# Part of the first statistics moved from VectorE to ScalarE: one ring piece of each of the last four images

## The chip, the cores and the metric

The kernel runs on one core of a Trainium2 chip. The core has five engines with a queue each: TensorE (PE in the profile; PEld is its weight load), VectorE (DVE), ScalarE (ACT), GpSimd (POOL) and SyncE (SP, which here only issues transfers). Every engine works through its own list in order and waits on semaphores for the others. On-chip memory is SBUF (128 partitions) and PSUM, where TensorE writes. The metric is the device time of one execution in microseconds; lower is better.

## The reference

The input `x` is 16 images of 128 channels and 64x64 pixels, in fp32. Two layers follow each other:

```
def _gn(v, G=32, eps=1e-5):                 # group norm: 4 channels a group
    g = v.reshape(B_, G, C_ // G, H_, W_)
    m = mean(g, axis=(2, 3, 4)); s = var(g, axis=(2, 3, 4))
    return ((g - m) / sqrt(s + eps)).reshape(v.shape)

x = x + diagonal_lstm(_gn(x))
x = x + quantum_conv(_gn(x))
```

The diagonal LSTM skews each image, so that row i starts i columns later, and scans the columns: the gates of a row at one step come from its own input, from its own hidden state and from that of the row above. The second layer maps the 128 channels of each pixel to 4 angles, simulates a 4-qubit circuit, and maps 4 expectations back to 128 channels. What matters here is the first `_gn`: before the scan can begin, the mean and the variance of each image's groups must be known, over all of `x`.

## The kernel before

**Stages.** In a first stage (to about 104 us) all of `x` is read once and its statistics are taken, while the weights are transposed and a small recurrence for rows that still wait is run. The second stage is the scan, some 1200 us. The third computes the second layer and writes the output.

**Pieces.** An image's 4096 pixels a channel are cut into eight pieces of 512. Five go into the tile `ring`, where the scan needs them; three go into passing buffers, `rest` (three buffers) and `spare[0..3]`, only to be summed. `rows(b)` issues the five transfers, `behind(b)` the three, all on SyncE's queue. At turn `b` of the loop over images (L369 on) `rows(b + 2)` and `behind(b + 1)` are issued.

**Statistics.** `statistics(b, k)` is one `bn_stats` on VectorE over piece `k` of image `b` (L283). It writes six numbers into `stats[:, b, k]`: count, mean and sum of squared deviations, for two halves. `aggregated(b)` (L286) joins the eight sixes of an image into a mean and a variance, `mv1[:, b]`. At turn `b` VectorE takes the five ring pieces of image `b + 1`, then the three passing pieces of image `b`, then the aggregate of `b`.

**The waiting rows.** Rows of the image to which the skewed scan has not come yet see no input, but their gates have a bias, so their state moves in a known way, the same for each such row. `inv_step(j)` computes one step of that, 33 in all, two or three a turn: four TensorE products (L194), four activations on ScalarE (L197), three small GpSimd operations (L200 to L202), two more activations (L204, L205), which give `hinv`. Each step waits for the one before. After each, two `keep` products (L177) are issued, whose results nobody reads; they only keep TensorE working.

**The end of the stage.** GpSimd copies columns of `hinv` into `hst[0]`, the scan's first hidden state (L398, L399). TensorE then runs the scan's first products on it (L404), three more `keep` products on buffers of the last images, and then `group_mean`, a product of the means with a group-averaging matrix (`gm`, L142). VectorE turns that into `mean1` (L143), `var1` follows, a second product (`gv`, L422), and `inverse_root` gives `rstd1` (with a square root on ScalarE, L149, whose table is loaded before it). With these GpSimd normalises the first scan inputs (L564 to L574).

**Buffers.** `spare` is eight tiles of 128x512. `spare[0..3]` hold weights and then passing pieces, `spare[4..5]` are `xns`, the normalised inputs of even and odd scan steps, `spare[6..7]` are `hst`. All four of the last are zeroed on GpSimd early in the stage:

```
for v in (*hst, *xns, none):
    nc.gpsimd.memset(v, 0.0)
```

**What sets the order.** The whole stage is under a manual schedule: each engine runs its instructions in the order in which the code writes them; only the waits are put in by the framework.

Of the kernel before, what the change touches and what calls it, by code (L numbers as in the profile page):

```python
# [11 lines left out]
F32 = mybir.dt.float32  # L12
AF = mybir.ActivationFunctionType
# [3 lines left out]
P = 128  # L17
NB = 16
# [7 lines left out]
BLOCK = ROWS * NW  # L26
CHUNK = 2 * BLOCK
# [53 lines left out]
def kernel(  # L81
# [16 lines left out]
    nc = tc.nc  # L98
# [10 lines left out]
    ring = const.tile([P, RING // ROWS, NB, BLOCK], F32, name="ring")  # L109
# [11 lines left out]
    mean2 = const.tile([P, NB], F32, name="mean2")  # L121
    rstd2 = const.tile([P, NB], F32, name="rstd2")
# [3 lines left out]
    spare = [const.tile([P, CHUNK], F32, name=f"spare{i}") for i in range(8)]  # L126
# [8 lines left out]
    def block(r):  # L135

        return (r + AHEAD if r < SLOTS else r - SLOTS) // ROWS
# [17 lines left out]
    small = ctx.enter_context(tc.tile_pool(name="small", bufs=2))  # L155
    with ExitStack() as scan:
# [5 lines left out]
        bias = wpool.tile([P, 4], F32, name="bias")  # L162
# [4 lines left out]
        xns, hst = ([v.rearrange("p (q n) -> p q n", q=2) for v in spare[i : i + 2]] for i in (4, 6))  # L167
        none = state.tile([P, NB], F32, name="none")
        gates = scan.enter_context(tc.tile_pool(name="gates", bufs=1))
        spool = scan.enter_context(tc.tile_pool(name="spool", bufs=1))  # L170
        stats = spool.tile([P, NB, NG2, 6], F32, name="stats")
        ps_small = scan.enter_context(tc.tile_pool(name="ps_small", bufs=1, space=PSUM))

        def keep(pool, tag, v):

            ps = pool.tile([P, v.shape[-1]], F32, name=nc.get_next_instruction_name(), tag=tag)
            nc.tensor.matmul(ps, lhsT=wsT[:, 0:P], rhs=v, start=True, stop=True)  # L177
# [8 lines left out]
        def inv_step(j, pool):  # L186


            ps = {}
            rhs = hinv[:, j : j + 1].to_broadcast([P, P])  # L190
            for g in ORDER:
                ps[g] = pool.tile([P, P], F32, name=f"inv_ps{j}_{g}", tag=f"inv{g}")
                w = wsT[:, g * 128 : (g + 1) * 128]
                nc.tensor.matmul(ps[g], lhsT=w, rhs=rhs, start=True, stop=True)  # L194
            ac = small.tile([P, 4], F32, name=f"inv_a{j}", tag="inv_a")
            for g in ORDER:
                nc.scalar.activation(ac[:, g : g + 1], ps[g][:, 0:1], FUNC[g], bias=bias[:, g : g + 1])  # L197
            ig = small.tile([P, 2], F32, name=f"inv_i{j}", tag="inv_i")
            c = cinv[:, j + 1 : j + 2]
            nc.gpsimd.tensor_mul(ig[:, 0:1], ac[:, GF : GF + 1], cinv[:, j : j + 1])  # L200
            nc.gpsimd.tensor_mul(ig[:, 1:2], ac[:, GI : GI + 1], ac[:, GG : GG + 1])
            nc.gpsimd.tensor_add(c, ig[:, 0:1], ig[:, 1:2])  # L202
            th = small.tile([P, 1], F32, name=f"inv_t{j}", tag="inv_t")
            nc.scalar.activation(th, c, AF.Tanh)  # L204
            nc.scalar.activation(  # L205
                hinv[:, j + 1 : j + 2], th, AF.Identity, scale=ac[:, GO : GO + 1]
            )
# [7 lines left out]
        with ExitStack() as prep:  # L215
# [15 lines left out]
            post_n = pp.tile([P, 4], F32, name="post_n")  # L231
            ident = pp.tile([P, P], F32, name="ident")
            mv1 = pp.tile([P, NB, 2], F32, name="mv1")
            bias8 = pp.tile([P, 8], F32, name="bias8")
            co = gates.tile([P, 8, 8], F32, name="co")
            cur = gates.tile([P, 2, 16], F32, name="amp_in")
# [6 lines left out]
            def rows(b):  # L243
                for k in ORDERED:
                    at = (2 * k * ROWS - AHEAD) * NW if k else SLOTS * NW
                    nc.sync.dma_start(
                        out=ring[:, 2 * k : 2 * k + 2, b, :],
                        in_=xv[b, :, at : at + CHUNK].rearrange("c (k n) -> c k n", n=BLOCK),
                    )

            def behind(b):
                rests[b] = []
                for i, k in enumerate(range(RING * NW, NH * NW, CHUNK)):
                    n = (3 * b + i) % 7
                    if n < 3:
                        rest = rest_pool.tile([P, CHUNK], F32, name=f"rest{b}_{k}", tag="rest")
                    else:
                        rest = spare[n - 3]
                    nc.sync.dma_start(out=rest, in_=xv[b, :, k : k + CHUNK])
                    rests[b].append(rest)  # L260
# [20 lines left out]
            def statistics(b, k):  # L281
                v = ring[:, 2 * k : 2 * k + 2, b, :] if k < 5 else rests[b][k - 5]
                nc.vector.bn_stats(stats[:, b, k, :], v)  # L283

            def aggregated(b):
                nc.vector.bn_aggr(  # L286
                    mv1[:, b, :], stats[:, b, 0:8].rearrange("p g s -> p (g s)")
                )
# [19 lines left out]
            def coefficients():  # L308
                nc.gpsimd.tensor_mul(co[:, 0], trig[:, 0, 0, :], trig[:, 0, 2, :])
                nc.gpsimd.tensor_mul(co[:, 1], trig[:, 1, 0, :], trig[:, 0, 2, :])  # L310
                nc.gpsimd.tensor_mul(co[:, 2], trig[:, 0, 1, :], trig[:, 1, 2, :])
                nc.gpsimd.tensor_mul(co[:, 3], trig[:, 1, 1, :], trig[:, 1, 2, :])
                nc.gpsimd.tensor_scalar_mul(co[:, 4:8], co[:, 0:4], -1.0)
                nc.gpsimd.tensor_copy(cur[:, 0], expand)
                nc.gpsimd.memset(cur[:, 1], 0.0)


            def transposed(name, to, of):
                tp = ps_prep.tile([P, 512], F32, name=f"{name}_ps", tag="tp")
                for g in range(4):  # L320
                    nc.tensor.transpose(tp[:, g * 128 : (g + 1) * 128], of(g), ident)
                nc.scalar.copy(to, tp)
# [30 lines left out]
            for k in (1, 2):  # L353
                statistics(0, k)
            for i in range(2):
                v = ws_n[i]
# [1 line left out]
            transposed("wsT", wsT, lambda g: sum_n[:, g, :])  # L358
            biases()
            coefficients()  # L360
            for v in (*hst, *xns, none):
                nc.gpsimd.memset(v, 0.0)
            nc.gpsimd.memset(w_image, 0.0)

            for k in (3, 4, 0):
                statistics(0, k)


            between = [angle_weights, output_weights]  # L369
            done = 0  # L370
            for b in range(NB):
                while b < NB - 1 and done * (NB - 1) < EARLY * (b + 1):
                    inv_step(done, ps_inv)
                    keep(ps_keep, "keep", ring[:, 2, b, 0:P])
                    keep(ps_keep, "keep", wsT[:, 0:P])
                    if done == 0:

                        transposed("wxT", wxT, lambda g: wx_n[:, g, :])
                        transposed("w0T", w0T, lambda g: ws_n[g // 2][:, g % 2, 0::2])
                        transposed("w1T", w1T, lambda g: ws_n[g // 2][:, g % 2, 1::2])  # L380
                    elif done > 4 and between:
                        between.pop(0)()
                    done += 1
                if b + 2 < NB:
                    rows(b + 2)
                if b + 1 < NB:
                    behind(b + 1)
                    for k in ORDERED:
                        statistics(b + 1, k)
                for k in (5, 6, 7):  # L390
                    statistics(b, k)
                aggregated(b)
            prep_ps.close()


            ps_gate = scan.enter_context(tc.tile_pool(name="ps_gate", bufs=7, space=PSUM))
# [468 lines left out]
        with tc.manual_schedule():  # L865
# [26 lines left out]
            v = ring[:, block(NH - ROWS)].rearrange("p i (r w) -> p i r w", w=NW)[:, :, :, NW - STRIP :]  # L892
            d, sq = (work.tile([P, NB, ROWS, STRIP], F32, name=f"strip{i}", tag=f"both{i}") for i in range(2))
            m = mean2.unsqueeze(2).unsqueeze(3).to_broadcast([P, NB, ROWS, STRIP])
# [7 lines left out]
            m = small.tile([P, NB], F32, name="m2", tag="gn_m")  # L902
# [84 lines left out]
    def sines(b, c=None):  # L987

        if b not in turns:
            turns[b] = sinp.tile([P, CHUNK], F32, name=f"y{b}", tag="y")  # L990
        y = half(turns[b], c)
        nc.scalar.activation(y, ths[b, c], AF.Identity, bias=b_image[:, b : b + 1])  # L992
        near = half(nearp.tile([P, CHUNK], F32, name=f"near{b}_{c}", tag="near"), c)
        nc.vector.tensor_scalar(near, y, ROUND, ROUND, ALU.add, ALU.subtract)  # L994
        nc.vector.tensor_sub(y, y, near)  # L995
        yield
        nc.scalar.activation(y, y, AF.Sin, scale=TWO_PI)
# [67 lines left out]
    with tc.manual_schedule():  # L1065
# [18 lines left out]
        later = sines(1)  # L1084
# [8 lines left out]
        later = sines(2)  # L1093
# [6 lines left out]
        for b in range(1, NB):  # L1100
            po = outputs(b, 0)
            later = sines(b + 2) if b + 2 < NB else iter(())
# [50 lines left out]
```

## Time and profile before

| | us |
|---|---|
| median of 3 runs (lowest, highest) | 1413.59 (1413.12, 1415.5) |
| the profiled execution | 1412.49 |
| its span, first to last instruction | 1410.7 |
| busy in the span: PE, DVE, ACT, POOL | 1352.7, 980.5, 778.7, 921.3 |
| busy from 20 to 95 us: PE, DVE, ACT, POOL | 59.01, 72.42, 45.51, 18.31 |
| moved from 20 to 95 us | 370 GB/s |

The table's first three rows are times of whole executions; the profile's span is that of its own execution, 1.79 us shorter than its time. Busy time is the sum of what an engine executed; issuing of transfers, waits and branches don't count. In an order-of-time view a line gives start, duration, engine, line of the code, operation, output and inputs by name with their shapes, how many instructions were joined, and in brackets how long the engine was idle before and what ended that.

### The profile page before, as it was taken

The numbers are of one execution on the slowest core, as the hardware profiler recorded it, in microseconds if no ns is written. First come the engines' busy times: TensorE is split into PE (matmuls) and PEld (weight loads), VectorE is DVE, ScalarE is ACT, GpSimd is POOL, SyncE is SP. The second block draws the span as 40 slices with busy tenths as digits, with TensorE's granted clock in tenths as the row PEclk, the third lists the DMA queues.
The fourth block names the chain that finished last, engine by engine and source line by source line (L and its number), as shares of the span: only waits on it lengthen the run. The fifth ranks groups of instructions, "written<-read, shape, count | busy, mean of one in ns | idle before, by whom it ended". The sixth has DMA issues, their size and how long they took to land. (4 is left out here: it accounts for less than half of the span.)

```text
span 1410.7 us, 20301 instructions
## 1 busy us (share of the span) xinstructions
PE 1352.7 (96%) x6030; PEld 962.4 (68%) x6030; DVE 980.5 (70%) x2549; ACT 778.7 (55%) x1860; POOL 921.3 (65%) x1823
## 2 busy tenths in 40 slices
PE   6778999999999999999999999999999999989996
PEld 5658887777777666666777777777767778786332
DVE  7993565566665666787777776766665566876996
ACT  4555666555555555555555555555555566654331
POOL 4226887777777667778888876777777667763300
PEclk9999999999999999999999999999999999999998
DMA  9980000000000000133333100000000000004999
GB/s 325 368 287 2 1 1 1 1 1 1 0 1 1 0 1 1 60 120 120 119 121 120 60 1 1 0 1 1 1 1 0 1 1 1 1 31 135 389 405 354
DMA packets 78926, 107.06 MB, mean 76 GB/s; under 512 B 5552, under 2 KB 53712, under 8 KB 78816
## 3 DMA queue, kind: packets, MB, share of 16 engines
q1 hardware_dynamic: 74176, 94.39, 19.2%
q0 software_dynamic: 3408, 10.58, 2.0%
q8 instruction: 48, 0.79, 0.2%
q10 hardware_dynamic: 1232, 0.80, 0.2%
q14 instruction: 62, 0.51, 0.1%
HBM read 59.61 MB, written 46.14 MB: 75 GB/s over the span
## 5 line engine op out<-in xcount | busy, mean ns | idle before, releaser
L583 PE MATMUL ps<-spare,wxT 128*128 128x512 f32 (+18 forms) x1280 | 479.6, 517 | 0.7 <-POOL spare L574 0.7
L767 DVE TENSOR_TENSOR ps<-ps,both 128x256 f32<-128x256 f32 (+9 forms) x544 | 221.6, 408 | 305.1 <-PE ps L752 303.7
L771 ACT ACTIVATE ps<-ps,bias 128x512 f32<-128x512 f32 (+23 forms) x480 | 279.3, 583 | 220.2 <-DVE ps L767 183.7
L752 PE MATMUL ps<-spare,w1T 128*128 128x256 f32 (+16 forms) x1272 | 345.8, 353 | 9.8 <-DVE spare L834 4.9
L583 PEld LDWEIGHTS ps<-spare,wxT 128*128 128x128 f32 x1280 | 230.9, 190 | 173.2 <-issue 155.5
L752 PE MATMUL ps<-spare,w0T 128*128 128x256 f32 (+16 forms) x1272 | 343.8, 352 | 0.8 <-POOL spare L608 0.8
L802 ACT COPY both<-ps 128x256 f32<-128x256 f32 (+9 forms) x544 | 191.6, 355 | 180.8 <-PE ps L752 161.2
L617 POOL TENSOR_TENSOR ring<-ring,spare 128x256 f32<-128x256 f32 (+8 forms) x487 | 247.8, 540 | 31.2 <-DVE stats L705 21.1
L752 PEld LDWEIGHTS ps<-spare,w1T 128*128 128x128 f32 x1272 | 229.8, 190 | 35.7 <-DVE spare L834 7.6
L752 PEld LDWEIGHTS ps<-spare,wsT 128*128 128x128 f32 x1088 | 194.9, 190 | 86.3 <-DVE spare L834 34.7
L752 PE MATMUL ps<-spare,wsT 128*128 128x256 f32 (+14 forms) x1088 | 241.3, 365 | 5.4 <-DVE spare L834 3.6
L752 PEld LDWEIGHTS ps<-spare,w0T 128*128 128x128 f32 x1272 | 230.3, 190 | 22.1 <-POOL spare L608 0.9
L574 POOL TENSOR_TENSOR spare<-spare,rstd 128x512 f32<-128x512 f32 (+10 forms) x160 | 171.0, 1069 | 14.8 <-DVE rstd L153 2.3
L569 POOL TENSOR_TENSOR spare<-ring 128x256 f32<-128x256 f32 (+8 forms) x213 | 147.2, 701 | 0.0
L828 ACT ACTIVATE g<-cst 128x256 f32<-128x256 f32 (+20 forms) x320 | 103.0, 368 | 64.3 <-DVE cst L827 63.7
L834 DVE TENSOR_TENSOR spare<-g,ps 128x256 f32<-128x256 f32 (+17 forms) x319 | 105.4, 368 | 44.0 <-ACT g L828 42.1
L564 POOL TENSOR_TENSOR spare<-ring,mean 128x16 f32<-128x16 f32 (+8 forms) x247 | 130.9, 539 | 6.2 <-DVE mean L143 6.0
L608 POOL TENSOR_TENSOR spare<-spare 128x240 f32<-128x240 f32 (+9 forms) x136 | 102.7, 755 | 29.5 <-DVE spare L834 25.7
L771 ACT ACTIVATE g<-ps,bias 128x512 f32<-128x512 f32 (+20 forms) x160 | 97.4, 609 | 27.1 <-DVE ps L767 21.3
L854 POOL COPY spare<-spare 128x16 f32<-128x16 f32 x64 | 21.1, 330 | 134.1 <-DVE spare L834 134.1
L827 DVE TENSOR_TENSOR cst<-cst,ps 128x256 f32<-128x256 f32 (+20 forms) x320 | 104.3, 367 | 5.5
L824 DVE TENSOR_TENSOR ps<-ps,g 128x512 f32<-128x512 f32 (+20 forms) x160 | 95.1, 594 | 17.0 <-ACT g L771 16.6
(368 smaller groups left out, 1097.2 us busy)
## 6 DMA issues: line engine op xcount, KB each, us to landing
out_dram<-ring SPq DMA_DIRECT2D x94, 256.0 KB, 5.1
ring<-in_x_dram SPq DMA_DIRECT2D x80, 256.0 KB, 5.6
low<-ring SPq DMA_DIRECT2D x6, 2048.0 KB, 7.5
ring<-in_x_dram SPq DMA_DIRECT2D x6, 2048.0 KB, 8.1
spare<-in_x_dram SPq DMA_DIRECT2D x27, 256.0 KB, 5.5
rest<-in_x_dram SPq DMA_DIRECT2D x21, 256.0 KB, 5.6
ring<-low POOLq DMA_DIRECT2D x19, 256.0 KB, 7.0
out_dram<-spare SPq DMA_DIRECT2D x14, 256.0 KB, 6.0
```

The lines of the kernel that those rows point to most:

```text
L564: nc.gpsimd.tensor_sub(by_pairs(xn, 0, j, n), x0, over(mean1, n))
L569: nc.gpsimd.tensor_sub(by_pairs(xn, 1, j, n), lower, of)
L574: nc.gpsimd.tensor_mul(v, v, r)
L583: nc.tensor.matmul(ps[g][:, :, a:b], lhsT=wxT[:, g * 128 : (g + 1) * 128], rhs=xns[t % 2][:, :, a:b], start=t > 0, stop=True, skip_group_c ...
L617: engine.tensor_add(x1, x1, by_pairs(new, q, j, n))
L752: nc.tensor.matmul(out, lhsT=w[:, g * 128 : (g + 1) * 128], rhs=rhs, start=False, stop=True, skip_group_check=True,)
L767: nc.vector.tensor_add(v, v, both[g][:, a:b])
L771: nc.scalar.activation(to[:, :, a:w], ps[g][:, :, a:w], FUNC[g], bias=bias[:, g : g + 1])
L802: nc.scalar.copy(both[g][:, a:b], ps[g][:, 0, a:b])
L827: nc.vector.tensor_add(c[:, q], c[:, q], ig[:, q])
L828: nc.scalar.activation(th[:, q, a:w], c[:, q], AF.Tanh)
L834: nc.vector.tensor_mul(new[:, q, a:v], th[:, q, a:v], act[GO][:, q, a:v])
```

## The change

The first ring piece (k = 0) of images 12 to 15 is no longer taken by `bn_stats`. The new generator `beside(b)` has ScalarE pass over it twice, once with Identity and once with Square, each time of (m - x), where m is a mean that `bn_stats` found for piece 1 of the same image; the accumulator outputs, the sum and the sum of squares, go into a column of `mean2` and `rstd2`, tiles that are unused at that time. Six small GpSimd operations then turn them into the six numbers of `stats[:, b, 0]`. The elementwise results of the passes are written to `spare[5]` and not read.

For images 12 to 14 the passes are spread over the steps of the waiting rows, one after each; the GpSimd operations (an "entry") come with the step after the second pass. After the 33rd step of the waiting rows follow the second pass of image 14, and, at turn 14, its entry and both passes and the entry of image 15. The aggregate of an image waits in a list, `whole`, until its entry is there, so the aggregate of 12 moves to the end of turn 13, and that of 13 to turn 14. Because `spare[5]` is `xns[1]`, its zeroing moves from the beginning of the stage to the place after the loop, ahead of the copies to `hst` on GpSimd.

```diff
+            unused = spare[5]
+            def beside(b):
+                v = ring[:, 0:2, b, :]
+                to = unused.rearrange("p (k n) -> p k n", n=BLOCK)
+                m = stats[:, b, 1, 1:2]
+                for i, f in enumerate((AF.Identity, AF.Square)):
+                    nc.scalar.activation(to, v, f, bias=m, scale=-1.0, accum_out=(mean2, rstd2)[i][:, b : b + 1])
+                    yield
+                d, q = mean2[:, b : b + 1], rstd2[:, b : b + 1]
+                t = small.tile([P, 2], F32, name=f"beside{b}", tag="beside")
+                e = stats[:, b, 0].rearrange("p (h s) -> p h s", s=3)
+                nc.gpsimd.tensor_scalar_mul(t[:, 0:1], d, 1.0 / CHUNK)
+                nc.gpsimd.tensor_sub(e[:, :, 1], m.to_broadcast([P, 2]), t[:, 0:1].to_broadcast([P, 2]))
+                nc.gpsimd.tensor_mul(t[:, 1:2], t[:, 0:1], d)
+                nc.gpsimd.tensor_sub(t[:, 1:2], q, t[:, 1:2])
+                nc.gpsimd.tensor_scalar_mul(e[:, :, 2], t[:, 1:2].to_broadcast([P, 2]), 0.5)
+                nc.gpsimd.tensor_copy(e[:, :, 0], stats[:, b, 1, 0::3])
...
-            for v in (*hst, *xns, none):
+            for v in (*hst, xns[0], none):
                 nc.gpsimd.memset(v, 0.0)
...
+            shared = set(range(NB - 4, NB))
+            passes, images, entries, whole = [], [], [], []
...
             for b in range(NB):
+                if b in shared and b < NB - 1:
+                    later = beside(b)
+                    passes += [later, later]
+                    images.append(b)
                 while b < NB - 1 and done * (NB - 1) < EARLY * (b + 1):
                     inv_step(done, ps_inv)
+                    while entries:
+                        next(entries[0][1], None)
+                        shared.discard(entries.pop(0)[0])
+                    if passes:
+                        later = passes.pop(0)
+                        next(later)
+                        if later not in passes:
+                            entries.append((images.pop(0), later))
...
                     for k in ORDERED:
-                        statistics(b + 1, k)
+                        if k or b + 1 not in shared:
+                            statistics(b + 1, k)
+                if b == NB - 2:
+                    later = beside(b + 1)
+                    for later in (entries.pop(0)[1], later, later, later):
+                        next(later, None)
+                    shared.clear()
                 for k in (5, 6, 7):
                     statistics(b, k)
-                aggregated(b)
+                whole.append(b)
+                while whole and whole[0] not in shared:
+                    aggregated(whole.pop(0))
             prep_ps.close()
+            nc.gpsimd.memset(xns[1], 0.0)
```

## The prediction

> **What bounds the kernel now.** The page first: a span of 1410.7 us, TensorE busy 96% of it, but that is an average over three stages; the change lies wholly in the first 104 us. So the next view was the busy time by stretch, and its rows for the end of that stage.
>
> ```profile
> 80.00:90.00 10.00, 7.48 (x48) 5.95 (x48) 9.84 (x17) 6.08 (x26) 2.32 (x12) 1.00 1.08 370
> 95.00:101.00 6.00, 5.07 (x25) 3.20 (x26) 5.38 (x11) 1.05 (x1) 0.12 (x2) 1.00 0.44 169
> ```
>
> After the stretch and its length come PE, PEld, DVE, ACT and POOL busy, the granted clock, the DMA share and GB/s. Two resources are full at once: VectorE at 9.84 of 10 us, and the DMA engines at a share of 1.08 and 370 GB/s. To see which leads, I asked what the issuing queue waited for from 20 to 95 us.
>
> ```profile
> SPq L246 <- DMA ring<-in_x_dram: 20.3, 61, 0.4
> SPq L259 <- DMA spare<-in_x_dram: 5.2, 21, 0.3
> SPq L259 <- DVE stats L283: 2.2, 3, 1.3
> ```
>
> The queue waits for earlier transfers; for VectorE it waits 2.2 us in all, and in the part from 70 us on, where images 12 to 15 lie, 0.5 us. The last three transfers, of image 15, were issued at 92.25, 93.0 and 93.7 us and took 5.5, 5.4 and 5.2 us to land: the last landed at 98.9. Now the same end in order of time, on all engines.
>
> ```profile
> 93.85 0.49 PE L177 MATMUL I-1361_1362<-wsT 128*128 128x128 f32 x2
> ...
> 94.46 0.29 ACT L205 ACTIVATE hinv<-inv_t,inv_a 128x1 f32<-128x1 f32 x1
> 94.77 1.28 ACT L149 ACT_TABLE_LOAD   x1
> ...
> 94.94 0.18 POOL L399 COPY spare<-hinv 128x1 f32<-128x1 f32 x1
> ...
> 95.17 0.49 PE L404 MATMUL ps<-spare,w1T 128*128 128x128 f32 x2 [0.83 <-POOL spare L399]
> ...
> 98.14 1.81 DVE L283 BATCH_NORM_STATS2 stats<-spare 128x6 f32<-128x512 f32 x3
> ...
> 98.90 0.91 PE L177 MATMUL I-1407_1408<-spare,wsT 128*128 128x384 f32 x2
> 99.99 0.37 DVE L286 BATCH_NORM_AGGREGATE mv<-stats 128x2 f32<-128x48 f32 x1
> ...
> 100.46 0.37 PE L142 MATMUL gm<-mv,wide_sb 128*128 128x16 f32 x2 [0.65 <-PE I-1407_1408 L177]
> ```
>
> Two strands meet in the group mean `gm` at 100.46. One is VectorE: the last `bn_stats` begins near 99.3, 0.4 us behind the landing of its data, and the aggregate ends at 100.36. The other is TensorE in its own order: the recurrence of waiting rows ends with `hinv` at 94.75 (ScalarE), GpSimd copies it to `hst`, 16 passes of L404 begin at 95.17, then three keep-busy products end at 99.81. That second strand has only 0.65 us to spare.
>
> **What the Trainium skill says.** "ScalarE: Activation LUTs", What ACT_TABLE_LOAD costs: an ACTIVATE with a pointer bias takes about 280 ns + 0.833 ns per column, and neighbours overlap by about 93 ns. For 512 columns that is 707 ns; this trace's nearest row (L992, Identity with bias, 128x512) has 687 ns, so it agrees. "VectorE: DVE Perf Modes", Two Vector instructions with no wait between them: an operation that writes out its accumulator is two instructions. That is said of VectorE; that ScalarE does likewise no row of this trace shows. "TensorE: Matmul & The Clock Gate", Part 1: after an idle window of some 3.4 us the clock is halved, and a busy window must pass before it returns; the windows run freely. The trace agrees in kind:
>
> ```profile
> 17.01 1.91 PE L194 MATMUL inv_ps<-hinv,wsT 128*128 128x128 f32 x8
> ...
> 22.45 1.16 PE L194 MATMUL inv_ps<-hinv,wsT 128*128 128x128 f32 x8 [0.47 <-ACT hinv L205]
> ```
> ```profile
> 1397.00:1398.00 1.00, 0.19 (x1) 0.00 (x0) 1.00 (x3) 0.00 (x0) 0.00 (x0) 1.00 1.02 391
> 1399.00:1400.00 1.00, 0.00 (x0) 0.00 (x0) 0.30 (x1) 0.00 (x0) 0.00 (x0) 0.58 1.04 389
> ```
>
> The same eight matmuls take 1.65 times as long before 20 us as after. At the end of the kernel the granted clock fell to 0.5 at about 1399.2, 2 us after the last matmul.
>
> **The change, part by part.**
>
> *Removed from VectorE:* four `bn_stats` of piece 0 (images 12 to 15), 0.68 us a row each, 0.65 apart: 2.6 us. Their worth is bounded by the landings. The pieces still land when they did, less at most the 0.5 us the queue waited for VectorE. Third rest piece of image 14: issued at 91.5, 5.6 us, so 97.1, where VectorE took it at once before. It then runs two aggregates (13 and 14) instead of one, 0.29 us more, before image 15's three pieces. VectorE ends at about 100.65 (100.36 + 0.29); without that shift at 99.7 to 99.9. So this strand gives between -0.7 and +0.3 us; I take +0.3.
>
> *Added to ScalarE:* eight passes over 128x512, each 0.70 us, plus an accumulator read. For the read no row exists: 0 if it is hidden, 0.29 if it is like the dearest 128x1 row (L205); I take 0.2. No table load is added in the new order. Five passes (both of 12, both of 13, first of 14) stand between `hinv` of one step and the next step's activations. ScalarE idles 0.58 us there; a pass starts 0.09 before the end of L205 and is over 0.14 us after the activations were due, and those four then run closer (0.72 us back to back at 12.56, 0.93 now). That leaves about 0.05 us a step, 0.25 in all; bounds 0 and 1.0.
>
> *Taken from GpSimd's start:* one of the four memsets at 11.77, 0.47 us. GpSimd's first L200 (14.39) stands behind them while its ScalarE input was ready at 13.3, so the recurrence starts up to 0.47 us earlier; some is lost to products still slow before 20 us. I take -0.25 (0 to -0.47). With the line above: `hinv` still ends at 94.75.
>
> *GpSimd entries of 12 and 13:* six small operations, 0.27 us where one needs the last and 0.13 where not, 1.2 us, in the 1.54 us in which GpSimd waits in each step. Nothing; with that cover gone, 1.2 us each.
>
> *The tail, where three passes, two entries and a memset are put ahead of the copies to `hst`.* ScalarE: 14's second pass with its read from 94.66 to 95.56, 15's first to 96.5 (its ring piece was issued near 89.5, took 5.6 us, landed at 95.1: no wait), 15's second to 97.43. Image 14's entry finishes in between, so VectorE, at aggregate 14 near 98.1, doesn't wait. Image 15's entry: last three operations at 97.5, 97.77, 97.90. Then the moved memset, 98.03 to 98.5 (0.53 us a row, 0.47 apart); then the three copies at 98.5, 98.63, 98.76, done at 98.94; before, they were done at 95.12. Queued behind them, in TensorE's order, are the 16 L404 passes, the three keep products and only then `gm`. L404 starts at 98.99 instead of 95.17. From there to the end of the last keep product is 99.81 - 95.17 = 4.64 us, so `gm` comes at 103.63, not 100.46: **+3.2 us**, with VectorE long done. ScalarE's table load moves from 94.77 to 97.4 and ends at 98.7, before the root needs it.
>
> *The clock.* TensorE's last product before the wait ends near 94.34, and nothing is queued until 98.99: 4.65 us of idling in place of 0.83. That is more than the 2 us after which the clock fell at the kernel's end, and more than one window. The products that follow then run 1.65 times as long until a busy window has passed, 3.4 to 6.8 us by the skill's window (at the start, products nearly unbroken from 16.09 went fast at 20.0, 3.9 us). Each slow us does 1/1.65 of its work, a loss of 0.39 us: 1.3 to 2.7, I take **2.0**.
>
> *Sum:* 3.2 + 2.0 = +5.2 us. Nothing later makes it up: the recurrence over diagonals starts from `gm`. The profiled execution took 1412.49 us (span 1410.7 and 1.79 around it): 1417.7. The median of the runs is 1.1 above the profiled one: 1413.59 + 5.2 = **1418.8**.
>
> **Rivals.**
>
> *Late, but the clock stays.* For it: the windows run freely, and a gap of 4.65 us need hold a whole idle one only in (4.65 - 3.4)/3.4, some 37% of placements. Against: at the end 2 us were enough. +3.2: 1416.8; 2.1 to 5 with the bounds (three reads at 0 and the full 0.47 us at the start, or reads of 0.29 and a late recurrence).
>
> *Not slower: VectorE and the landings set `gm`.* That holds if L404 begins by 95.8, so that its 4.64 us end at 100.46 as before. It then gains up to 0.7 us: 1412.9, and no more, for the last landing at 98.9 holds VectorE. For it: VectorE is the last releaser of `gm` now. Against: three passes of 0.70 us after 94.66 alone end at 96.7.
>
> *Much worse: the recurrence slows too.* If reads are long and each step slips 0.4 us (5 steps, 2 us), and TensorE stays slow through all 4.64 us (7.7 instead), `gm` is 8 us late: 1421.6.
>
> **How the numbers follow.** A measurement tells about 0.2%, 2.8 us, from no change, so slower begins at 1416.4. Forecast (late and slow clock) 0.62, +4 to +7, all slower. Late, clock stays: 0.25; 0.15 slower, 0.10 same. Not slower: 0.07; 0.05 same, 0.02 faster. Much worse: 0.06. Slower 0.83, same 0.15, faster 0.02. Low end 1415.6 takes in the lower bound of the second case; high end 1421.0 the slow clock's with late reads; outside lie most of the last two cases.
>
> **What the profile after would show.** L404's successor starts near 99.0, released by GpSimd, after 4 us or more of idle TensorE; `gm` waits for the keep product with VectorE done 3 us earlier; the granted clock shows 0.5 around 97 to 103, and the L404 passes take 0.39 us a pair if it didn't fall, 0.63 if it did. VectorE ends near 100.6. The read shows as a second ScalarE instruction. The forecast is wrong if the passes are far from 0.9 us, or if the clock stays.

## The result, and the profile after

The changed kernel takes 1417.49 us (median of 7 runs, 1416.91 to 1420.63), the kernel before 1413.12 us (7 runs, 1412.28 to 1415.5). The ratio is 1.0033 with a 95% interval of 1.0024 to 1.0042: slower by 4.7 us (3.4 to 5.9). The forecast was 1418.8 us, range 1415.6 to 1421.0. The profiled execution took 1418.0 us, its span is 1416.2.

The end of the first stage after the change, in order of time, TensorE's part:

```profile
92.35 0.49 PE L177 MATMUL I-1376_1377<-wsT 128*128 128x128 f32 x2
98.39 0.79 PE L451 MATMUL ps<-spare,w1T 128*128 128x128 f32 x2 [5.55 <-POOL spare L446]
...
101.54 0.63 PE L451 MATMUL ps<-spare,w0T 128*128 128x128 f32 x2
101.96 1.49 PE L177 MATMUL I-1433_1434<-rest,wsT 128*128 128x384 f32 x2
103.51 0.91 PE L177 MATMUL I-1436_1437<-rest,wsT 128*128 128x384 f32 x2
104.48 0.91 PE L177 MATMUL I-1439_1440<-spare,wsT 128*128 128x384 f32 x2
105.45 0.40 PE L142 MATMUL gm<-mv,wide_sb 128*128 128x16 f32 x2
```

TensorE idles 5.55 us, released by GpSimd's last copy to `hst` (L446 now). The first scan products begin at 98.39 (95.17 before), and their pairs take 0.63 us (0.39 before). `gm` follows the last keep product without a gap, at 105.45 instead of 100.46: 4.99 us late. That lateness is carried through unchanged: the last `gm` of the second statistics begins at 1290.5 against 1285.6. VectorE had been done long before, as its own order shows:

```profile
98.10 1.81 DVE L285 BATCH_NORM_STATS2 stats<-spare 128x6 f32<-128x512 f32 x3
100.02 0.37 DVE L308 BATCH_NORM_AGGREGATE mv<-stats 128x2 f32<-128x48 f32 x1
105.88 0.17 DVE L143 TENSOR_SCALAR mean<-gm 128x16 f32<-128x16 f32 x1 [5.49 <-PE gm L142]
```

Its last aggregate ends at 100.39, against 100.36 before: four `bn_stats` fewer, and nothing won. The tail on ScalarE and GpSimd that held the copies:

```profile
92.95 0.29 ACT L205 ACTIVATE hinv<-inv_t,inv_a 128x1 f32<-128x1 f32 x1
93.16 0.70 ACT L295 ACTIVATE spare<-ring,stats 128x512 f32<-128x512 f32 x1
93.77 0.19 ACT L295 ACTIVATION_READ_ACCUMULATOR spare<-ring,stats 128x1 f32 x1
95.07 0.72 ACT L295 ACTIVATE spare<-ring,stats 128x512 f32<-128x512 f32 x1 [1.11 <-DVE stats L285]
...
95.92 0.72 ACT L295 ACTIVATE spare<-ring,stats 128x512 f32<-128x512 f32 x1
```
```profile
97.31 0.18 POOL L305 COPY stats<-stats 128x2 f32<-128x2 f32 x1
97.43 0.52 POOL L440 MEMSET spare<- 128x512 f32 x1
97.90 0.32 POOL L445 COPY spare<-hinv 128x16 f32<-128x16 f32 x2
98.15 0.18 POOL L446 COPY spare<-hinv 128x1 f32<-128x1 f32 x1
```

The recurrence is over at 93.24, yet the copies of its result run 4.7 us later, behind image 15's entry and the memset. Last, the granted clock (the column after POOL's busy time) by stretches:

```profile
96.00:98.00 2.00, 0.00 (x0) 0.00 (x0) 2.00 (x5) 1.98 (x3) 1.58 (x8) 0.64 0.87 334
102.00:103.00 1.00, 1.00 (x3) 0.30 (x2) 0.00 (x0) 0.00 (x0) 0.00 (x0) 0.50 0.00 0
103.00:104.00 1.00, 0.94 (x3) 0.30 (x2) 0.00 (x0) 0.00 (x0) 0.00 (x0) 0.80 0.00 0
```

The trace's clock records hold only 1 and 0.5, so a mean of 0.64 over two microseconds puts the fall at 96.56, and 0.80 over one puts the return at 103.4.

### The profile page after: what moved, and what is told of

Read it like the earlier page. It is cut to its first block, busy times and chain, and to the rows that moved or that the text cites. A ratio compares the mean times of both kernels' runs of the same rounds, so it can differ in the third digit from the quotient of the medians.

```text
span 1416.2 us, 20348 instructions
## 1 busy us (share of the span) xinstructions
PE 1353.1 (96%) x6030; PEld 962.6 (68%) x6030; DVE 978.8 (69%) x2545; ACT 783.6 (55%) x1876; POOL 925.9 (65%) x1847
## 5 line engine op out<-in xcount | busy, mean ns | idle before, releaser
L871 DVE TENSOR_TENSOR ps<-ps,g 128x512 f32<-128x512 f32 (+20 forms) x160 | 95.1, 594 | 17.0 <-ACT g L818 16.6
```

## The experiments

The theory: the loss is TensorE's strand, late because GpSimd's copies stand behind the tail, and slowed by the clock that falls while it idles; VectorE's relief is worth nothing, since the landings hold it. Rivals: the passes on ScalarE or the entries cost the time themselves; lateness alone, without the clock; VectorE bounds the stage.

**The copies moved ahead of the tail** (one move in the changed kernel):

```diff
                 if b == NB - 2:
+                    for r, v in ((0, hst[0][:, 0, 0:NB]), (EARLY, hst[0][:, 0, NB : NB + 1])):
+                        nc.gpsimd.tensor_copy(v, hinv[:, r : r + 1].to_broadcast(list(v.shape)))
+                    nc.gpsimd.tensor_copy(hst[0][:, 1, NB : NB + 1], hinv[:, EARLY : EARLY + 1])
                     later = beside(b + 1)
...
-            for r, v in ((0, hst[0][:, 0, 0:NB]), (EARLY, hst[0][:, 0, NB : NB + 1])):
-                nc.gpsimd.tensor_copy(v, hinv[:, r : r + 1].to_broadcast(list(v.shape)))
-            nc.gpsimd.tensor_copy(hst[0][:, 1, NB : NB + 1], hinv[:, EARLY : EARLY + 1])
```

> The change with one thing moved: GpSimd's three copies of hinv to hst are issued before the entries of images 14 and 15 instead of behind them and the memset. Theory (TensorE's strand, held by GpSimd, and its clock make the loss): the first scan products begin near 93.5 us, the group mean waits for VectorE again and comes at 100.4 to 101 us; the time is within 1 us of before, 1412.5 to 1414. Rival (the loss is in the passes on ScalarE or the two aggregates together on VectorE): the time stays near 1417.5, +4.4 on before.

Measured: 1413.59 us, ratio to before 1.0001 (0.9993 to 1.0010). The whole loss is gone, with all eight passes, all four entries and the memset still there. That rules out the first rival. TensorE's order in this run:

```profile
93.64 0.49 PE L451 MATMUL ps<-spare,w1T 128*128 128x128 f32 x2 [0.83 <-POOL spare L432]
...
98.41 0.91 PE L177 MATMUL I-1439_1440<-spare,wsT 128*128 128x384 f32 x2
100.86 0.41 PE L142 MATMUL gm<-mv,wide_sb 128*128 128x16 f32 x2 [1.54 <-issue]
101.12 1.63 PE L177 MATMUL I-1449_1450<-wxT,wsT 128*128 128x384 f32 x2
```

The strand is now early; `gm` comes just after VectorE's end at 100.76. The keep product behind `gm` takes 1.63 us instead of 0.89: the clock fell here too, at 101.0, after an idle gap of only 1.54 us.

**Keep products in the gap** (five more in the changed kernel, nothing else):

```diff
                 if b == NB - 2:
+                    for _ in range(5):
+                        keep(ps_keep, "keep", wxT[:, 0 : 3 * P])
                     later = beside(b + 1)
```

> The change with five more keep-busy products of 128x384 on TensorE after the last step of the waiting rows, in the 5.55 us in which it idled. Theory (late strand plus clock): the clock stays, the first scan products still begin near 98.4 us but take 1.9 us and the three keep products 2.75, so the group mean comes at 103.0 in place of 105.45; the time is 2.6 us above before and 2.4 below the change: the clock's share is 2.4. Rival (lateness alone): no gain over the change, +4.4 to +5.0 on before.

Measured: 1415.94 us, 1.0021 (1.0014 to 1.0028), +3.0 us on before. The clock stays at 1.00 from 20 to 1400 us, and the strand from the first scan product to `gm` takes 4.70 us, where the change has 7.06 (98.39 to 105.45):

```profile
99.37 0.49 PE L453 MATMUL ps<-spare,w1T 128*128 128x128 f32 x2 [1.58 <-POOL spare L448]
...
104.07 0.40 PE L142 MATMUL gm<-mv,wide_sb 128*128 128x16 f32 x2
```

So the clock's share in the profile is 2.36 us, as expected. Between the times it is 1.7 us (0.0033 less 0.0021), with intervals that just overlap. In this profile image 15's data landed later, and the first scan products began 1.0 us after those of the change; whether that is so in most executions is not shown. The +3.0 us that stay are lateness. The times' own runs agree on the clock: the mean clock of a whole run, recorded to 0.001, is 0.991 to 0.993 in all seven of the change and 0.994 to 0.996 in all 21 of `fill`, as in the kernel before; 6.84 us at half clock are 0.0024 of a run.

**Only the removal** (the kernel before without the four `bn_stats`, nothing in their place; the aggregates of these images lack piece 0):

```diff
-                        statistics(b + 1, k)
+                        if k or b + 1 < NB - 4:
+                            statistics(b + 1, k)
...
-                    mv1[:, b, :], stats[:, b, 0:8].rearrange("p g s -> p (g s)")
+                    mv1[:, b, :], stats[:, b, (b >= NB - 4) : 8].rearrange("p g s -> p (g s)")
```

> The kernel before with the four bn_stats of piece 0 of images 12 to 15 left out and nothing in their place: the statistics of these images lack that piece. Theory (the landings hold the stage): VectorE ends 0 to 0.7 us sooner, the time changes by 0 to -0.7 us. Rival (VectorE bounds the stage): -2.6 us, four times 0.65.

Measured: 1412.75 us, 0.9992 (0.9984 to 1.0000): -1.1 us (0 to -2.3), the medians 0.5 apart. The -2.6 us of the rival lies outside the interval. In the trace VectorE now stands and waits for transfers:

```profile
95.83 1.97 DVE L283 BATCH_NORM_STATS2 stats<-rest 128x6 f32<-128x512 f32 x3 [0.73 <-DMA rest<-in_x_dram]
...
99.94 0.34 DVE L286 BATCH_NORM_AGGREGATE mv<-stats 128x2 f32<-128x42 f32 x1
```

It ends at 100.28 instead of 100.36. From 70 us to its end it idles 3.07 us (27.21 busy of 30.28), before 0.51 (29.85 of 30.36): the four saved instructions, 2.6 us, became waiting.

**Only the delay** (the kernel before with extra memsets of `xns[1]` ahead of the copies, eight and then four):

```diff
             prep_ps.close()
+            for _ in range(8):
+                nc.gpsimd.memset(xns[1], 0.0)
```

> The kernel before with eight extra memsets of 128x512 (0.47 us each, 3.8 us) on GpSimd ahead of the copies to hst; no passes on ScalarE. Theory: the first scan products begin at 98.9 us, the clock falls in the 4.6 us gap, and the group mean comes near 105.6 (103.6 if the clock stays): +3.1 to +5.1 us on before. Rival (the passes and entries themselves cost the time): within 0.5 us of before.

Measured with eight: 1418.01 us, 1.0032 (1.0020 to 1.0043), +4.5 us. A delay of the copies alone, without any of the change's work, gives the change's whole loss. The first scan products wait for the copies, and `gm` follows late:

```profile
99.23 0.79 PE L406 MATMUL ps<-spare,w1T 128*128 128x128 f32 x2 [4.82 <-POOL spare L401]
...
106.43 0.40 PE L142 MATMUL gm<-mv,wide_sb 128*128 128x16 f32 x2
```

> The kernel before with four extra memsets of 128x512 on GpSimd ahead of the copies to hst (0.58 us each in the run delay8, 2.3 us). Theory: the first scan products begin near 97.0 us after a gap of some 2.7 us; the lateness alone makes the group mean 1.2 us late (101.7); with a fallen clock 2.5 to 3.5 us. Rival (the clock falls only after a gap of 3.4 us or more): +1.2 us in every run.

Measured with four: 1414.47 us, 1.0007 (1.0000 to 1.0013), about +1.0 us. The profile shows 2.50 us of idling, first products at 96.02, the clock falling at 96.7 and returning at 100.1, `gm` at 102.37:

```profile
96.02 0.49 PE L406 MATMUL ps<-spare,w1T 128*128 128x128 f32 x2 [2.50 <-POOL spare L401]
...
96.89 0.64 PE L406 MATMUL ps<-spare,w0T 128*128 128x128 f32 x2
```

The fourth pair is the first that is slow throughout. So in this execution the clock fell after a gap shorter than 3.4 us, and the rival fails there. The times don't refute it: +1.0 us is nearer to the rival's +1.2 than to the 2.5 to 3.5 expected with a fallen clock, and the profiled execution, at 1415.87 us, is the longest of the 21 (1412.95 to 1415.87). In how many of the others the clock fell is open.

**The memset behind the copies** (in the changed kernel):

```diff
             prep_ps.close()
-            nc.gpsimd.memset(xns[1], 0.0)
...
             nc.gpsimd.tensor_copy(hst[0][:, 1, NB : NB + 1], hinv[:, EARLY : EARLY + 1])
+            nc.gpsimd.memset(xns[1], 0.0)
```

> The change with the memset of the odd scan input moved behind the copies to hst on GpSimd. Theory: the copies, the first scan products and the group mean come 0.5 us sooner, the clock falls all the same: +3.9 to +4.5 us on before, 0.5 below the change. Rival (the memset's place matters by more, as cause of the late strand): +1 us or less on before.

Measured: 1417.85 us, 1.0034 (1.0021 to 1.0046); the expected 0.5 us is not seen. In this profile image 15's piece landed 0.7 us later, so the copies, though they start only 0.12 us behind the start of the entry's last operation instead of 0.59, ended at 98.59 against 98.33. From the first pass of image 15 to the end of the copies it is 2.80 us (95.79 to 98.59) against 3.26 in the change (95.07 to 98.33), so in the trace the memset's 0.5 us is gained. The memset is a small part of the delay at most; whether its 0.5 us counts in the time is open.

**Images 12 to 14 only:**

```diff
-            shared = set(range(NB - 4, NB))
+            shared = set(range(NB - 4, NB - 1))
...
-                    later = beside(b + 1)
-                    for later in (entries.pop(0)[1], later, later, later):
-                        next(later, None)
+                    next(entries.pop(0)[1], None)
```

> The change for images 12 to 14 alone: image 15's first piece goes back to bn_stats, so the last two passes, their wait for image 15's rows and the last entry are gone; the memset stays ahead of the copies. Theory: the entry of image 14 ends near 94.7 us, the memset at 95.2, the first scan products begin near 95.7, the group mean comes at 100.4 to 101 (102 if the clock falls in a gap of 2.9 us): 0 to +1.5 us on before. Rival (image 15's part is not what costs): +4.4 us.

Measured: 1414.31 us, 1.0008 (1.0001 to 1.0014), +1.1 us. By the difference of the two, image 15's two passes and its entry carry 3.6 of the 4.7 us. Here the first scan products begin at 96.05 after 2.77 us of idling, the clock falls at 95.5 and returns at 98.9, and `gm` comes at 102.11.

**Copies ahead and one more keep product before `gm`** (shown against `copies_first`):

```diff
+            keep(ps_small, "small", wxT[:, 0 : 3 * P])
             group_mean(ps_small, mv1[:, :, 0], mean1, 1, 1.0)
```

> The copies moved ahead as in the run copies_first, and one more keep-busy product of 128x384 (0.97 us) right ahead of the group mean, in the 1.5 us in which TensorE idled there and after which its clock had fallen. Theory: the clock stays at full through the group mean and the products behind it; the group mean comes with VectorE's end near 100.4 to 100.9 us and the first full scan products 3.5 us later as before; the time is 0.4 to 0.6 us below copies_first, 1412.5 to 1413.3. Rival (the fall of the clock there costs nothing): the same as copies_first.

Measured: 1413.15 us, 1.0001 (0.9993 to 1.0009). The times don't tell it from `copies_first` (the same ratio), so the 0.4 to 0.6 us expected are not seen there; the traces do: the clock stays, the keep product behind `gm` takes 0.89 us again, and the first full scan products begin 3.48 us after `gm` instead of 3.95. In this trace the first pass of image 15 is put down to the transfer for which it waited:

```profile
95.51 0.72 ACT L295 ACTIVATE spare<-ring,stats 128x512 f32<-128x512 f32 x1 [1.58 <-DMA ring<-in_x_dram]
```

Neither this nor any other version that was run is faster than the kernel before by more than the measurement tells.

## Why the prediction was right

**The bound.** Right. The landings hold VectorE: its end was put between 0.7 us sooner and 0.3 later, at 100.65 in the likeliest; it came at 100.39. The removal alone gave 0.1 us in the trace. Which landing holds it was read a little wrong: not the last one, at 98.9, which VectorE takes up 0.4 us later, but that of image 14's third passing piece. It landed at 97.10 before and 97.08 in `removal`, VectorE took it at once in both, and had no wait from there to its end.

**The tail.** The order was right: passes, entries, memset, copies, first scan products, keep products, `gm`. Its parts: passes 0.70 to 0.72 us (0.70 predicted), the read a second instruction of 0.19 us, half of it beside the pass (0.2 on top was put down), the memset 0.52 with the copies 0.47 behind its start. But the term at its start was mis-sized. The recurrence was to end at 94.75 and ended at 93.24. The five passes slowed it by nothing (its steps are 2.39 us with and without them, where 0.05 each was put down), and more was won at its beginning than the memset's 0.47 us: the products of its second step took 1.06 us in place of 1.91. That second part is luck of the execution. In the runs with nothing changed at the start, they took 1.91 (before), 1.92 (`delay8`), 1.06 and 1.06 (`delay4`, `removal`), and the last step's products began at 92.41, 92.48, 91.60 and 91.58; the clock rose at 20.2, 19.4, 14.8 and 13.9 us. So an execution in which it rises sooner has 0.8 us more. The tail did not get all of the 1.5 us, because "no wait" for image 15's ring piece no longer held: the piece landed at 94.96, near the 95.1 foreseen, and ScalarE, earlier than foreseen, stood 1.11 us until 95.07. So the passes began 0.5 us earlier than the 95.6 predicted, and the first scan products 0.6 earlier, at 98.39 against 98.99.

What set the tail was therefore the landing of image 15's last ring piece, not the end of the recurrence. The profile puts this wait down to VectorE, whose fourth `bn_stats` ended at 95.01. But in all five traces with this wait (the change, `copies_first`, `fill`, `memset_last`, `copies_warm`) the pass begins 0.11 us after the landing, while from the end of that `bn_stats` it is 0.05 us in one and up to 0.13 in others; and three of the five name the transfer.

**The sum.** Lateness: 3.2 predicted. The first scan products were 3.22 late (98.39 - 95.17), of which the spare time before `gm` took up 0.59 (5.29 us from them to `gm` before, 4.70 at full clock without waiting): 2.63. Clock: 2.0 predicted, 2.36 measured (7.06 less 4.70). The slow stretch was 5.0 us long, from 98.39 to 103.4, inside the 3.4 to 6.8 foreseen; the loss per slow us was taken as 0.39 from the products of a step of the recurrence and was 0.47, since the 16 scan passes took 3.57 us for 1.89. Together 4.99 for 5.2 predicted: that the sum is nearer than its terms, 0.6 too much lateness and 0.4 too little clock, is luck. Of the 1.3 us between the forecast of 1418.8 and the measured median, 0.5 lie in the base, a median of three runs (1413.59) where seven gave 1413.12.

**The rivals.** The clock fell, so "late, but the clock stays" is out for the profiled run, and `fill` shows what it would have been: +3.0 us. "Not slower" would have needed first scan products by 95.8; `copies_first` has them at 93.64 and is as fast as before. "Much worse" needed a recurrence slowed by the passes, which it wasn't.

**The chance put on the clock** was argued from a wrong criterion: that a gap has to hold a wholly idle window. In the change's profile it did hold one; the next section but one tells what shorter gaps did. The other argument, the fall 2 us after the kernel's last matmul, is no price either: in `removal` the clock fell at 1396.30, before the modelled end of the last matmul at 1396.36.

## What to carry to other kernels

When work moves off a busy engine, ask first whether that engine or its data sets the end: here VectorE was 98% busy (9.84 of 10 us) and still had nothing to give, because it read as fast as the transfers landed. Then follow the moved work in the queue of its new engine to whatever stands behind it: three tiny copies behind a late entry held 16 matmuls and a group mean. And TensorE, made to wait, paid twice here, for the wait and for the slow clock after it; small filler products saved the second part (`fill`), and the order of GpSimd's queue both (`copies_first`).

## What the runs showed that was not expected

TensorE's clock can fall after much less than a wholly idle window. Falls and returns lie on a grid: 96.56 and 103.40 in the change (6.84 apart), 96.68 and 100.10 in `delay4` (3.42), 95.52 and 98.92 in `three` (3.40), 101.04 and 104.44 in `copies_first` (3.40). So a window of about 3.4 us seems to decide, and it runs on by itself: the clock's first rise, which the clock records also hold, came at 14.66 us in the change and at 14.77 in `delay4`, in both cases 24 such windows of 3.41 us before the fall.

The busy time in the window that ended with a fall, by the modelled ends of the matmuls, was zero in the change, 27% in `delay4` (0.27 + 0.66 of 3.42 us), some 33% in `three` and some 53% in `copies_first` (1.82 us), with gaps of 5.55, 2.50, 2.77 and 1.54 us. So the wholly idle window that the prediction takes from the Trainium skill ("TensorE: Matmul & The Clock Gate", Part 1) is not needed here; where the two differ, the measurement decides.

Nor does the length of the gap alone decide: in `fill` TensorE idled 1.58 us before the first scan products, longer than in `copies_first`, and the clock stayed. Counted on in steps of 3.413 us from the clock's first rise in that trace (15.44 us), the whole gap lies in the window from 97.36 to 100.77, which is 54% busy (1.83 us). In the kernel before (first rise at 20.18) the window from 91.86 to 95.27 is 60% busy (2.05 us), and the clock stayed too. If the modelled busy time is the measure, the boundary lies near a half, an estimate from these few windows. Whether it is the whole measure is open: the fall in `removal` at 1396.30 came behind products that the profile models as unbroken.

The accumulator of a ScalarE activation costs a second instruction, `ACTIVATION_READ_ACCUMULATOR`, of 0.18 to 0.19 us, which begins some 0.09 us before the end of the pass.
